# A Perceiver layer on one core: the feed-forward stage in twelve tiles, with its head inside the last closing

## The chip, the cores and the metric

The kernel runs on one core of one Trainium2 chip. The metric is device time in microseconds: 2316.69 us is the median of three runs before the change (2315.12 to 2320.33). A core has five engines with instruction streams of their own: PE (matrix products; its weight loads are listed as PEld), DVE (vector), ACT (scalar functions), POOL (general) and SP, which here issues all DMA transfers. Each engine works through its stream in order. An instruction that waits for another engine or for a DMA holds up all that stand behind it on its own engine, and on SP those are the transfers of other parts of the kernel.

## What is computed

Three blocks on `x` of 16 x 32 tokens by 512, each behind a layer norm and with a residual: a graph block, a state-space scan with 128 heads in 8 groups, and a feed-forward block. The change is about the third. Its weight matrices are a quarter as wide as the layer and are repeated four times, and each has a rank-two addition:

```python
def _qlora_linear(x, wq, A, B):
    w = jnp.tile(wq, (1, 4))
    base = x @ w.T
    lora = x @ A.T @ B.T
    return base + lora * LORA_SCALING               # 0.5
gate = silu(_qlora_linear(x, w1q, a1, b1))      # 512 -> 1376
up = _qlora_linear(x, w3q, a3, b3)              # 512 -> 1376
x = x + _qlora_linear(gate * up, w2q, a2, b2)   # 1376 -> 512
```

Since the weights repeat, `x @ w.T` is the sum of the four quarters of `x`, times the small matrix: one product with 128 rows in place of four.

## The kernel before

**The scan** (`scan_part`, L1116) runs in an order written out by hand (`manual_schedule`, L1258): each engine gets its instructions in the order of the Python code. The loop over groups (L1493) does for each of 8 steps i: the projections of the next group (`gate`, `current`, both through `project`, L1175, whose weights come by SP into six buffers of the tag `win`), and for the present group `turn` (transposes, decays; it also issues the load of a `wo` tile), `outputs` (PE products `py`) and `gated` (DVE, ACT and, on POOL, the sum of squares `ssq`). POOL also makes `da` (`spread`, L1275), which PE needs for `pl` (`decays`). A group ends with a closing: 32 products of 128x512 with the output weights, in four blocks q of 128 tokens, and an addition to `xt` per block (`close`, L1466; for the first six groups `close_by_seven`). `close` yields in the middle and at the end of each block. The closing of group 6 is woven into the steps of group 7; that of group 7 runs by itself.

**The rank-two parts** (`LowRank`, L130) are done in bf16: an f32 operand is split into three bf16 parts (`split`: eight DVE operations), and the products of the parts stand in 18 rows, multiplied by masks (`masks`). `load` fetches and splits the three `b` matrices in ten pieces; it is a generator that `current` advances by one piece per step from the loop of group 0 on. Its first piece makes the masks, issues the loads `lw` on SP (nine per piece) and clears the tiles on POOL; each further one splits the piece before and loads the next.

**The feed-forward stage** (`ffn_part`, L1522) begins when the scan has ended, in pools of its own, and its order is chosen by the framework's scheduler. Its **head**: six weight loads, layer norm of the four blocks of `xt` (ACT's Ln and Exp, each with a table load), 16 transposes, the sum `vs` of the four quarters, and the rank-two products `pa` of the values with `a1` and `a3` (18 columns, 512 tokens) with their splits. Its **tiles**: 16 tiles of 86 hidden units; for each two f32 products (L1580), two bf16 products of the rank-two part (L1589), Silu on ACT, the product on DVE, a third f32 product with `a2` into 18 columns (L1597), and from tile 4 on the addition into one of four sums. Its **output**: the split of the third low-rank sum, 16 f32 products with `w2` and four bf16 ones (L1605, L1606), four additions of the residual (L1608) and four stores.

Of the kernel before, what the change touches and what calls it, by code (L numbers as in the profile page):

```python
# [8 lines left out]
F32 = mybir.dt.float32  # L9
F16 = mybir.dt.float16  # L10
BF16 = mybir.dt.bfloat16
# [32 lines left out]
TG = NT // G_M  # L44
HT = 86
NHT = 16
LR = 18
LEAD = 6
PREP = (49, 46, 42)
# [4 lines left out]
def kernel(ctx: ExitStack, tc: tile.TileContext, I, out):  # L54
# [67 lines left out]
    late = ctx.enter_context(tc.tile_pool(name="late", bufs=1))  # L122
    lows = LowRank(nc, tc, late, I)
    with ExitStack() as cx:
        scan_part(nc, tc, cx, I, id32, ones, xt, U, rstd, lows)
    with ExitStack() as cx:
        ffn_part(nc, tc, cx, I, id32, xt, layernorm, lows, out)


class LowRank:  # L130

    def __init__(self, nc, tc, const, I):
        self.nc, self.tc, self.I = nc, tc, I
        self.weights = {
            n: const.tile([P, w], BF16, name=f"lb{n}") for n, w in (("1", HT * NHT), ("3", HT * NHT), ("2", D))
        }
        self.values = {n: const.tile([P, D], BF16, name=f"lv{n}") for n in ("1", "3", "2")}  # L140

        self.of = [const.tile([LR, 3], F32, name=f"lof{k}") for k in range(2)]

    def masks(self, pool):
        nc = self.nc
        t = pool.tile([LR, 3, 3], F32, name="lmask")
        for k, pat, width in ((0, [[-6, 3], [0, 3]], 6), (1, [[-2, 3], [-6, 3]], 2)):
            nc.gpsimd.memset(t, 1.0)
            nc.gpsimd.affine_select(
                out=t, in_=t, compare_op=ALU.is_ge, fill=0.0, base=0, pattern=pat, channel_multiplier=1  # L150
            )
            nc.gpsimd.affine_select(
                out=t, in_=t, compare_op=ALU.is_ge, fill=0.0, base=width - 1,
                pattern=[[-a, b] for a, b in pat], channel_multiplier=-1,
            )
            if k == 0:
                nc.vector.tensor_copy(self.of[0], t[:, :, 0])
            else:
                nc.vector.tensor_reduce(self.of[1], t, AX.X, ALU.add)

    def split(self, pool, dst, src, of, key):

        nc = self.nc
        n = src.shape[-1]
        for k in range(3):
            p = pool.tile([LR, n], BF16, tag="lp", name=f"lp{key}_{k}")
            nc.vector.tensor_copy(p, src)  # L167
            if k < 2:
                nc.vector.tensor_tensor(src, src, p, ALU.subtract)  # L169
            if k == 0:  # L170
                nc.vector.tensor_scalar(dst, p, of[:, 0:1], None, ALU.mult)  # L171
            else:
                nc.vector.scalar_tensor_tensor(dst, p, of[:, k:k + 1], dst, ALU.mult, ALU.add)  # L173

    def load(self, pool, width=344):
        nc = self.nc
        self.masks(pool)
        for t in (*self.weights.values(), *self.values.values()):
            nc.gpsimd.memset(t, 0.0)
        for n, t in self.weights.items():  # L180
            for c in range(0, t.shape[-1], width):
                cols = slice(c, min(c + width, t.shape[-1]))
                w = pool.tile([LR, width], F32, tag="lw", name=f"lw{n}_{c}")[:, :cols.stop - c]
                for k in range(9):
                    nc.sync.dma_start(out=w[2 * k:2 * k + 2], in_=self.I[f"b{n}T"][:, cols])
                yield
                self.split(pool, t[:LR, cols], w, self.of[1], f"b{n}_{c}")


def node_orders(nc, pool, tmp, ps, X, idx, id32, nid, own, others):  # L190
# [922 lines left out]
            pass  # L1113


def scan_part(nc, tc, cx, I, id32, ones, xt, u, rstd, lows):  # L1116


    sc = cx.enter_context(tc.tile_pool(name="sconst", bufs=1))
# [373 lines left out]
    for g in range(G_M):  # L1493
        mix = Mix(g)
        conv = None
        for i in range(TG):
            if g + 1 < G_M:
                gate(g + 1, i)
            end_of(conv)
            conv = None  # L1500
            if i:
                mix.gated(i - 1)
            mix.turn(i)
            if g + 1 < G_M:
                conv = current(g + 1, i)
                next(conv)
            else:
                next(last, None)
            mix.summed(i)
            mix.outputs(i)  # L1510
# [3 lines left out]
            mix.summed(TG)  # L1514
        end_of(last)
        last = mix.closing()
        if g + 2 != G_M:
            end_of(last)
            last = None


def ffn_part(nc, tc, cx, I, id32, xt, layernorm, lows, out):  # L1522


    fc = cx.enter_context(tc.tile_pool(name="fconst", bufs=1))
    wk = cx.enter_context(tc.tile_pool(name="fwk", bufs=2))
    sm = cx.enter_context(tc.tile_pool(name="fsm", bufs=3))
    ps = cx.enter_context(tc.tile_pool(name="fps", bufs=2, space=PSUM))
    ps1 = cx.enter_context(tc.tile_pool(name="fps1", bufs=1, space=PSUM))
    NH = HT * NHT  # L1530
    w = {}
    for name, shape in (
        ("a1T", [P, 4, 2]), ("a3T", [P, 4, 2]), ("a2T", [HT, NHT, 2]), ("w1T", [P, NH]), ("w3T", [P, NH]),
        ("w2T", [HT, 4, D]),
    ):
        w[name] = fc.tile(shape, F32, name=f"f_{name}")
        nc.sync.dma_start(out=w[name], in_=I[name])
        if name[0] == "a":

            t = fc.tile([shape[0], shape[1], LR], F32, name=f"f_{name}r")  # L1540
            nc.vector.tensor_copy(
                t.rearrange("p k (a r) -> p k a r", r=2),
                w[name].unsqueeze(2).to_broadcast([shape[0], shape[1], LR // 2, 2]),
            )
            w[name] = t

    v = fc.tile([P, 4, D], F32, name="v")
    for q in range(4):
        layernorm(sm, v[:, q], xt[:, q], f"ff{q}")
    vT = fc.tile([P, 4, D], F32, name="vT")  # L1550
    for k in range(4):
        pt = ps.tile([P, 4, P], F32, tag="t", name=f"fpt{k}")
        for q in range(4):
            nc.tensor.transpose(pt[:, q], v[:, q, k * P:(k + 1) * P], id32)  # L1554
        nc.scalar.copy(vT[:, k], pt.rearrange("p q t -> p (q t)"))  # L1555

    vs = fc.tile([P, D], F32, name="vs")
    nc.vector.tensor_tensor(vs, vT[:, 0], vT[:, 1], ALU.add)
    for k in (2, 3):
        nc.vector.tensor_tensor(vs, vs, vT[:, k], ALU.add)  # L1560
    def lower(n, pa):
        t = fc.tile([LR, D], F32, name=f"low{n}")
        nc.vector.tensor_scalar(t, pa, 0.5, None, ALU.mult)  # L1563
        lows.split(wk, lows.values[n][:LR], t, lows.of[0], f"v{n}")

    for n in ("1", "3"):
        pa = ps1.tile([LR, D], F32, tag="lo", name=f"pa{n}")
        for k in range(4):
            nc.tensor.matmul(pa, lhsT=w[f"a{n}T"][:, k], rhs=vT[:, k], start=(k == 0), stop=(k == 3))  # L1569
        lower(n, pa)  # L1570

    gsum = fc.tile([HT, 4, D], F32, name="gsum")
    pa2 = ps1.tile([LR, D], F32, tag="lo2", name="pa2")
    half = []

    def first(t):
        pp = {}
        for n in ("1", "3"):
            pp[n] = ps.tile([HT, D], F32, tag=f"p{n}", name=f"fp{n}_{t}")
            nc.tensor.matmul(pp[n], lhsT=w[f"w{n}T"][:, t * HT:(t + 1) * HT], rhs=vs, start=True, stop=False)  # L1580
        half.append(pp)

    first(0)
    for t in range(NHT):
        if t + 1 < NHT:
            first(t + 1)
        pp = half.pop(0)
        for n in ("1", "3"):
            nc.tensor.matmul(  # L1589
                pp[n], lhsT=lows.weights[n][:, t * HT:(t + 1) * HT], rhs=lows.values[n], start=False, stop=True  # L1590
            )
        sg = wk.tile([HT, D], F32, tag="sg", name=f"sg{t}")
        nc.scalar.activation(sg, pp["1"], AF.Silu)
        r = t % 4
        gt = gsum[:, r] if t < 4 else wk.tile([HT, D], F32, tag="gt", name=f"gt{t}")
        nc.vector.tensor_tensor(gt, sg, pp["3"], ALU.mult)
        nc.tensor.matmul(pa2, lhsT=w["a2T"][:, t], rhs=gt, start=(t == 0), stop=(t == NHT - 1))  # L1597
        if t >= 4:
            nc.vector.tensor_tensor(gsum[:, r], gsum[:, r], gt, ALU.add)
    lower("2", pa2)  # L1600
    for q in range(4):
        tq = slice(q * P, (q + 1) * P)
        po = ps.tile([P, D], F32, tag="t", name=f"fpo{q}")
        for r in range(4):
            nc.tensor.matmul(po, lhsT=gsum[:, r, tq], rhs=w["w2T"][:, r], start=(r == 0), stop=False)  # L1605
        nc.tensor.matmul(po, lhsT=lows.values["2"][:, tq], rhs=lows.weights["2"], start=False, stop=True)  # L1606
        o = wk.tile([P, D], F32, tag="fo", name=f"fo{q}")
        nc.vector.tensor_tensor(o, po, xt[:, q], ALU.add)  # L1608
        nc.sync.dma_start(out=out[tq, :], in_=o)


# [50 lines left out]
```

## Time and profile before

| | |
|---|---|
| median of three runs | 2316.69 us (2315.12 to 2320.33) |
| the profiled execution, first to last instruction | 2316.7 us |
| PE busy | 2131.8 us, 92% |
| DVE busy | 1835.5 us, 79% |
| ACT busy | 1140.4 us, 49% |
| POOL busy | 840.7 us, 36% |
| mean granted clock of PE | 0.977 |
| scan ends, feed-forward stage begins | about 2218 us |
| its first bf16 product | 2249.2 us |

How to read the profile. Its times are from the start of the span. In the timeline a line gives start, duration, engine, source line, operation, output<-inputs, and how many like instructions were merged; in brackets stands how long the engine was idle before and what released it. An f32 product shows as two records. In a table by stretches the columns are: stretch, its length, then the busy time of PE, PEld, DVE, ACT and POOL (with numbers of instructions), the clock granted to PE as a share of full speed, the busy share of the DMA engines, and GB/s. The ends of products are modelled.

### The profile page before, as it was taken

The numbers are of one execution on the slowest core, as the hardware profiler recorded it, in microseconds if no ns is written. First come the engines' busy times: TensorE is split into PE (matmuls) and PEld (weight loads), VectorE is DVE, ScalarE is ACT, GpSimd is POOL, SyncE is SP. The second block draws the span as 40 slices with busy tenths as digits, with TensorE's granted clock in tenths as the row PEclk, the third lists the DMA queues.
The fourth block names the chain that finished last, engine by engine and source line by source line (L and its number), as shares of the span: only waits on it lengthen the run. The fifth ranks groups of instructions, "written<-read, shape, count | busy, mean of one in ns | idle before, by whom it ended". The sixth has DMA issues, their size and how long they took to land. (4 is left out here: it accounts for less than half of the span.)

```text
span 2316.7 us, 89754 instructions
## 1 busy us (share of the span) xinstructions
PE 2131.8 (92%) x39522; PEld 1300.3 (56%) x39522; DVE 1835.5 (79%) x3974; ACT 1140.4 (49%) x2073; POOL 840.7 (36%) x897
## 2 busy tenths in 40 slices
PE   5599899999999998899999789989999999999979
PEld 2255555776557775567777544455646566464422
DVE  8488897999989999889999763788786967866643
ACT  6686667556675554455555222433353534435321
POOL 2156656455565565655655100111120202112200
PEclk9899999999999999999999799999999999999989
DMA  1324242231232322323212112112122121211100
GB/s 46 81 59 84 52 81 60 52 83 45 63 76 48 82 52 49 84 47 77 56 36 44 49 51 79 60 56 89 45 73 64 46 91 55 73 60 46 37 37 18
DMA packets 121629, 138.05 MB, mean 60 GB/s; under 512 B 18398, under 2 KB 79506, under 8 KB 121154
## 3 DMA queue, kind: packets, MB, share of 16 engines
q1 hardware_dynamic: 121240, 132.32, 22.5%
q8 instruction: 311, 5.10, 1.0%
q14 instruction: 78, 0.64, 0.1%
HBM read 77.02 MB, written 12.85 MB: 39 GB/s over the span
## 5 line engine op out<-in xcount | busy, mean ns | idle before, releaser
L890 POOL TENSOR_TENSOR EN<-e,rz 128x480 f32<-128x480 f32 x344 | 342.5, 996 | 499.4 <-DVE rz L888 410.2
L915 PE MATMUL u<-WA,DD 128*32 128x128 bf16 (+1 forms) x16512 | 414.1, 248 | 16.6 <-issue 16.4
L920 ACT COPY us<-u 128x512 f32<-128x512 f32 x516 | 302.1, 587 | 152.3 <-PE u L915 136.9
L915 PEld LDWEIGHTS <-DD 128*32 128x32 f16 x16512 | 338.6, 97 | 50.6 <-issue 48.1
L875 ACT ACTIVATE e<-s,smc 128x480 f32<-128x480 f32 x344 | 227.7, 662 | 252.6 <-PE s L870 222.0
L811 POOL TENSOR_TENSOR DD<-fs,crep 128x480 f16<-128x480 f32 (+2 forms) x344 | 349.6, 1017 | 0.0
L943 PEld LDWEIGHTS h<-e,us 128*32 128x32 f32 (+1 forms) x11008 | 246.0, 125 | 133.4 <-issue 66.6
L943 PE MATMUL h<-e,us 128*32 128x30 f32 (+1 forms) x11008 | 279.2, 210 | 31.3 <-issue 14.0
L1368 POOL TENSOR_TENSOR ssq<-ssq,sq 128x512 f32<-128x512 f32 x56 | 89.9, 1606 | 592.6 <-ACT sq L1367 592.6
L862 DVE TENSOR_REDUCE c<-s 128x16 bf16<-128x480 f32 x344 | 220.5, 641 | 83.8 <-PE s L853 80.4
L1181 PE MATMUL ppg<-hT,wing 128*128 128x512 f32 x512 | 238.3, 609 | 0.0
L1181 PE MATMUL ppch<-hT,winch 128*128 128x512 f32 x512 | 230.5, 592 | 0.0
L896 DVE STREAM_TRANSPOSE e<-EN 128x512 f32<-128x512 f32 x344 | 224.7, 653 | 0.0
L882 DVE TENSOR_REDUCE z<-e 128x16 f32<-128x480 f32 x344 | 219.6, 638 | 0.5 <-ACT e L875 0.4
L1194 DVE SCALAR_TENSOR_TENSOR cyh<-ppch,t_conv_w,cyh 128x496 f32<-128x496 f32 (+2 forms) x192 | 137.5, 716 | 99.9 <-ACT cyh L1188 95.3
L541 ACT ACTIVATE sgn<-kd 128x512 bf16<-128x512 f32 x256 | 153.1, 598 | 51.4 <-PE kd L540 48.3
L853 PEld LDWEIGHTS <-DD 128*32 128x32 f16 x5504 | 80.8, 96 | 158.2 <-issue 135.5
L751 DVE TENSOR_SCALAR oh<-it,rank 128x512 bf16<-128x512 f16 x512 | 155.8, 365 | 8.5 <-PE pp L705 8.5
L853 PE MATMUL s<-DX,DD 128*32 128x120 f16 x5504 | 142.3, 221 | 18.6 <-DMA DX<-DD 15.3
L1181 PEld LDWEIGHTS ppch<-hT,winch 128*128 128x128 f32 x512 | 94.5, 190 | 109.1 <-issue 102.5
L1181 PEld LDWEIGHTS ppg<-hT,wing 128*128 128x128 f32 x512 | 94.5, 192 | 107.0 <-issue 99.4
L870 PE MATMUL s<-c,idb 128*128 128x480 bf16 x344 | 130.4, 379 | 5.6 <-DVE c L862 2.7
(372 smaller groups left out, 3156.1 us busy)
## 6 DMA issues: line engine op xcount, KB each, us to landing
DX<-DD SPq DMA_DIRECT2D x456, 90.0 KB
wing<-in_in_proj SPq DMA_DIRECT2D x64, 256.0 KB
winch<-in_in_proj SPq DMA_DIRECT2D x64, 256.0 KB
wo<-in_out_proj SPq DMA_DIRECT2D x64, 256.0 KB
crep<-dC SPq DMA_DIRECT2D x128, 64.0 KB
dS<-so SPq DMA_DIRECT2D x32, 256.0 KB
fs<-dS SPq DMA_DIRECT2D x128, 64.0 KB
wincB<-in_in_proj SPq DMA_DIRECT2D x8, 256.0 KB
```

The costliest lines, as they stand in the source:

```text
L751: nc.vector.tensor_scalar(oh[:, j], it2, rank[:, c, m, 4 * g + b:4 * g + b + 1], None, ALU.is_equal)
L811: nc.gpsimd.tensor_tensor(d[:, :, m0 - n0:n1 - n0], win, crep[:, :, m0:n1].unsqueeze(3).to_broadcast([P, 4, n1 - m0, K]), ALU.subtract,)
L853: nc.tensor.matmul(s[rh, j * 4 * QB:(j + 1) * 4 * QB].rearrange("p (b q) -> p b q", b=4), lhsT=d[:, h, c0:c0 + 32], rhs=dx[:, h, :, c0:c0 ...
L862: nc.vector.tensor_reduce(c, live["s", at, gi].rearrange("p (i q) -> p i q", q=QB), AX.X, ALU.max, negate=True)
L875: nc.scalar.activation(e, s.rearrange("p (i q) -> p i q", q=QB), AF.Exp, scale=smc)
L882: nc.vector.tensor_reduce(z, e, AX.X, ALU.add)
L890: nc.gpsimd.tensor_tensor(en[:, :, :QB], e, rz.unsqueeze(2).to_broadcast([P, NI, QB]), ALU.mult)
L896: nc.vector.transpose(e.rearrange("p i q -> p (i q)"), en.rearrange("p i q -> p (i q)"))
L915: nc.tensor.matmul(u[rh, jj], lhsT=d[:, h, c0:c0 + 32], rhs=WA[k][:, h].rearrange("p b o -> p (b o)"), start=(jj == 0 and k == 0), stop=(k ...
L920: nc.scalar.copy(us[:, j - jj:j + 1], u)
L943: nc.tensor.matmul(h[r:r + co, pr, q0:q0 + QB], lhsT=us[:, j, b * co:(b + 1) * co], rhs=e[:, 4 * j + b, :QB], start=npair > 1, stop=True, ...
L1181: nc.tensor.matmul(pp, lhsT=w[:, k], rhs=hT[:, k], start=(k == 0), stop=(k == 3))
```

## The change

Four things are done.

1. **Twelve tiles.** The 1376 hidden units are taken as four repeats of 344, each in pieces of 128, 128 and 88 rows (`HC`). A piece c of repeat a is a tile. The four repeats of a piece are added, so the output needs three products per block, not four.
2. **Side by side.** The product with `a2` of the four tiles of a piece goes to four groups of 32 columns, into one bank (`pa2[rows]`), four in a row. The output's rank-two weights are copied to all four row groups. `a1` and `a3` stand in one operand of 64 columns, and the split values of both in one tile (`"13"`), `a3`'s at row 32.
3. **The head per block.** `ffn_part` is gone; a class `Ffn` stays in the scan's pools and in the order by hand. Block q-1 is transposed in the middle of closing block q and its rank-two product is done behind it, followed by the norm of block q. One ACT table with Ln and Exp is loaded ahead.
4. **Early fetches.** `fetch` loads all weights at the start of group 7's loop, into buffers of the scan, and spreads `a1`, `a3`, `a2` on POOL.

The masks and the `"2"` weights are copied to row groups 32, 64 and 96 by SBUF-to-SBUF DMAs on SP. The diff, cut to its core:

```diff
@@ LowRank.masks
+        for of in self.of:
+            for r in (32, 64, 96):
+                nc.sync.dma_start(out=of[r:r + LR], in_=of[:LR])
@@ LowRank.load
                 yield
-                self.split(pool, t[:LR, cols], w, self.of[1], f"b{n}_{c}")
+                self.split(pool, t[at, cols], w, at, self.of[1], f"b{n}_{c}")
+        t = self.weights["2"]
+        for r in (32, 64, 96):
+            nc.sync.dma_start(out=t[r:r + LR], in_=t[:LR])
@@ scan_part, loop over groups
+        if g + 1 == G_M:
+            fetched = fetch(nc, I, wpool, sm)
...
+    nc.scalar.preload_act_table_set("natural_log_exp_and_others")
+    for q in range(4):
+        next(last)
+        if q:
+            ffn.turn(q - 1)
+        next(last)
+        if q:
+            ffn.lower(q - 1)
+        ffn.norm(q)
+    ffn.rest()
+def fetch(nc, I, wpool, sm):
...
+            nc.sync.dma_start(
+                out=t[:, :, :rows], in_=I[f"w{n}T"].rearrange("p (a r) -> p a r", a=4)[:, :, r0:r0 + rows]
+            )
...
+    for c, to, k, rows in row_pieces():
+        nc.sync.dma_start(out=w["2"][c][to], in_=I["w2T"][rows, k])
+        nc.sync.dma_start(out=raw2[to, :, c], in_=by_k[rows, k])
+    a13 = sm.tile([P, 4, 64], F32, tag="osum", name="fa13", bufs=TG // 2)
+    nc.gpsimd.memset(a13, 0.0)
+    for n, at in (("1", 0), ("3", 32)):
...
+        nc.sync.dma_start(out=raw, in_=I[f"a{n}T"])
+        nc.gpsimd.tensor_scalar(
+            a13[:, :, at:at + LR].rearrange("p k (a r) -> p k a r", r=2),
+            raw.unsqueeze(2).to_broadcast([P, 4, LR // 2, 2]), 0.5, None, ALU.mult,
+        )
...
+    nc.gpsimd.memset(a2, 0.0)
+    for c, (_, rows) in enumerate(HC):
+        nc.gpsimd.tensor_scalar(
+            a2[:rows, :, c, :LR].rearrange("p k (a r) -> p k a r", r=2),
+            raw2[:rows, :, c].unsqueeze(2).to_broadcast([rows, 4, LR // 2, 2]), 0.5, None, ALU.mult,
+        )
+class Ffn:
...
+    def turn(self, q):
+        pt = self.bank("m", f"fpt{q}").rearrange("p (k t) -> p k t", k=4)
+        for k in range(4):
+            nc.tensor.transpose(pt[:, k], self.v[:, q, k * P:(k + 1) * P], self.id32)
+        nc.vector.tensor_reduce(self.vs[:, tq], pt.rearrange("p k t -> p t k"), AX.X, ALU.add)
+        nc.scalar.copy(self.vT[:, :, tq], pt)
+    def lower(self, q):
+        pa = self.bank("m", f"fpa{q}")[:64, :P]
+        for k in range(4):
+            nc.tensor.matmul(pa, lhsT=self.w["a13"][:, k], rhs=self.vT[:, k, tq], start=(k == 0), stop=(k == 3))
+        t = self.wk.tile([P, D], F32, tag="sq", name=f"flow{q}")[:64, :P]
+        nc.scalar.copy(t, pa)
+        self.lows.split(None, self.lows.values["13"][rows, tq], t, rows, self.lows.of[0], f"v{q}", self.part[:, :P])
+    def rest(self):
...
+        early, late = slice(0, 3 * P), slice(3 * P, D)
+        for t in range(2):
+            first(t, early, True)
+        self.turn(3)
+        nc.scalar.preload_act_table_set("silu_and_others")
+        for t in range(2):
+            first(t, late, False)
+        self.lower(3)
...
+        for t, (a, c) in enumerate(tiles):
+            for f, ph in zip(("1", "3"), pp):
+                nc.tensor.matmul(
+                    ph, lhsT=lows.weights[f][:, cols], rhs=lows.values["13"], start=False, stop=True,
...
+            if t + 2 < len(tiles):
+                first(t + 2, slice(0, D), True)
+            nc.scalar.activation(sg, pp[0], AF.Silu)
+            nc.vector.tensor_tensor(gt, sg, pp[1], ALU.mult)
...
+            if t + 1 == len(tiles):
+                base(0, 0)
+                base(0, 1)
+            for b, x in enumerate(gts):
+                rows = slice(32 * b, 32 * b + 32)
+                nc.tensor.matmul(
+                    pa2[rows], lhsT=w["a2"][:n, b, c], rhs=x, start=(c == 0), stop=(c == len(HC) - 1),
...
+            for x in gts[1:]:
+                nc.vector.tensor_tensor(gts[0], gts[0], x, ALU.add)
...
+        nc.scalar.copy(low, pa2)
+        lows.split(None, lows.values["2"], low, everything, lows.of[0], "v2", self.part)
+        base(1, 0)
...
+        base(1, 2)
+        for q in range(2, 6):
+            if q < 4:
+                for c in range(len(HC)):
+                    base(q, c)
+            for q in {2: (), 3: (0, 1), 4: (2,), 5: (3,)}[q]:
+                finish(q)
```

`first(t, ...)` makes the two f32 products of tile t in banks of the tags `p` and `y` (two each); `base(q, c)` is an f32 product with `w2`; `finish(q)` is the bf16 product, DVE's addition of the residual into a tile of the tag `ssq` (two buffers) and the store.

## Prediction

> **What bounds the kernel now.** The page's span, 2316.7 us, is that of the profiled execution, and the median of the runs shown, 2316.69 us, agrees with it, so every sum below is made against 2316.7. I read first the chain of waits that ended last: on its last 87 us it stands on PE in the feed-forward lines (L1580, L1589, L1597, L1605), before that on ACT and DVE. The busy times by stretch say what that means.
>
> ```profile
> 2200.00:2210.00 10.00, 10.00 (x25) 4.50 (x24) 1.50 (x2) 0.00 (x0) 0.00 (x0) 1.00 0.00 0
> ...
> 2220.00:2230.00 10.00, 1.80 (x6) 0.86 (x6) 4.58 (x27) 9.10 (x14) 0.00 (x0) 0.65 0.45 169
> 2230.00:2240.00 10.00, 8.11 (x20) 2.62 (x20) 3.93 (x9) 3.53 (x5) 0.00 (x0) 0.67 0.10 44
> ...
> 2260.00:2270.00 10.00, 9.93 (x26) 2.65 (x24) 3.40 (x6) 2.15 (x4) 0.00 (x0) 1.00 0.00 0
> ```
>
> PE (the first busy time) is full in the last closing and in the sixteen tiles, and nearly empty in the head between them, where ACT is full and the granted clock falls to 0.65. The timeline gives the tiles:
>
> ```profile
> 2261.23 1.03 PE L1589 MATMUL fp<-lv,lb 128*86 128x512 bf16 x4
> 2261.65 1.08 ACT L1593 ACTIVATE sg<-fp 86x512 f32<-86x512 f32 x2 [5.74 <-PE fp L1589]
> 2262.27 1.28 DVE L1596 TENSOR_TENSOR gt<-sg,fp 86x512 f32<-86x512 f32 x2 [5.54 <-PE fp L1589]
> 2262.29 1.09 PE L1580 MATMUL fp<-vs,f_w1T 128*86 128x512 f32 x2
> 2263.31 1.03 PE L1597 MATMUL pa<-gt,f_a2Tr 86*18 86x512 f32 x2
> ...
> 2268.05 1.03 PE L1589 MATMUL fp<-lv,lb 128*86 128x512 bf16 x4
> ```
>
> Two tiles take 6.82 us (2261.23 to 2268.05). An f32 product is two records of 0.43 us, a bf16 one a record of 0.215; a change between the 128x128 and the 18-column form costs 0.16 or 0.10 (2262.29 to 2263.31 is 1.02, not 0.86). Each tile pays a full 0.86 us product for 18 columns. Measured from S = 2189.10, where the last closing begins, the end is 127.6 us away: 28.6 closing, 31.5 head (to the first L1589 at 2249.16), 50 tiles, 17.5 output.
>
> **The change: the tail.** Blocks 1 to 3 of the closing now carry the head. Behind block q's last matmul PE does the rank-two product of q-1 (0.16 + 4 x 2 x 0.107 = 1.02), ACT copies it (0.28, by the 0.59 of a 512-column copy), DVE splits it (eight operations: 2.07 us at 168 columns from 1603.56, about 1.85 at 128 by the slope to 344), and only then runs block q's norm, 2.92 us as in the chain of 1313.65 to 1316.57 that has no table load. From the block's end: 1.02 + 0.23 drain + 0.3 + 1.85 + 2.92 + waits = 6.4. PE meanwhile has 1.02 and half a block (3.44 + 0.1), so it idles 1.9, then does four transposes (0.53) and the other half (3.44): 10.4 us a block where 6.87 stood. Block 0 ends at S + 6.97; the root, now without its 1.28 table load, and the first norm are ready at S + 13.3, so block 1 ends at S + 17.5, block 3 at S + 38.3. Behind it the last norm (6.3), transposes, sum of four (0.65), the late quarter of two tiles (0.86), the product, copy and split give 12.0: the first bf16 product comes at S + 50.3, where it stood at S + 60.1.
>
> Twelve tiles replace sixteen. But both of a tile's banks come from pools of two, and each tile's bf16 products are followed at once by the f32 products of tile t+2, which need the bank that tile t's Silu reads. By the rows above Silu starts 0.42 after the bf16 product, lasts 0.58, and PE starts 0.06 later: 1.06 instead of 0.43. The old order put two tiles' bf16 products there, and the wait was 0.04. A tile is 1.06 + 1.72 + 0.07 = 2.85; ten of them 28.5. DVE's products and additions (0.69 each, 4.8 us per four tiles) lie beside PE's 13.8; were that cover gone, each addition would cost its 0.69. The Silu table load (1.28) lies behind the last copy of the transposes, while PE does the late quarter.
>
> The rank-two sums run four side by side in 32-column groups. The nearest row is L1352, f32 on two groups of 64 columns: 16 records in 1.03 us (2151.56 to 2152.59) where 0.107 each would make 1.71. I read it as an overlap of neighbours in program order: a group's second record waits for its first, and the next group starts beside it. Four products then take five records, 2.15; ends are two records (0.87) and eight (3.44). With 0.26 of form changes, two of them give 4.8, then two bf16 products and two products of the output (2.8). From the third group on: 2.15, six f32 products around DVE's additions, six more, bf16, 11.4 in all; the split (4.2) lies beside these. Together 50.3 + 28.5 + 4.8 + 2.8 + 11.4 = 97.8 to the first output addition.
>
> The Trainium skill, "TensorE: Matmul & The Clock Gate", Part 3, gives packed tiles one product's span plus 4 ns for each further tile; by it a group is about 0.87 and the sum 3.8 us lower, an estimate; the same page says that matmuls start and end strictly in order, and no row here shows four f32 groups.
>
> The four additions now come in a row, and the output tile has two buffers. In the trace the third addition waited 3.4 us for the first store, which landed 4.4 after its issue; the last store took 3.0 when alone. So: two additions 1.4, the second pair from 5.1 on, 1.4, and a store among two, 3.5: 10.1. End: S + 107.9, 19.7 us earlier.
>
> Less the clock: between block 3 and the tiles PE has 2.2 us of work in 8.4. A similar hole cost:
>
> ```profile
> 1597.55 0.43 PE L1352 MATMUL py<-el,hd 128*64 128x128 f32 x2 [1.57 <-DVE el L1333]
> 1599.21 1.97 PE L1352 MATMUL py<-el,hd 128*64 128x128 f32 x14 [1.24 <-DVE el L1333]
> 1601.11 5.69 PE L1181 MATMUL ppg<-hT,wing 128*128 128x512 f32 x8
> ```
>
> The last line is 3.60 elsewhere. I take 2.5 (ends 0 and 7, if each block loses some): the tail gains **17.2**.
>
> **The change: the front.** Three edits add waits to in-order queues. SP before:
>
> ```profile
> 1446.81 2.71 SPq L185 DMA_DIRECT2D lw<-in_b1T  x9
> 1449.56 0.35 SPq L1343 DMA_DIRECT2D wo<-in_out_proj  x1
> 1450.02 0.38 SPq L1178 DMA_DIRECT2D winch<-in_in_proj  x1
> ...
> 1479.87 3.08 SPq L185 DMA_DIRECT2D lw<-in_b1T  x9
> ```
>
> The last line shows SP standing 18 us for DVE's split. `masks` now issues six copies on SP, just ahead of the nine at 1446.81, and they read what DVE writes here:
>
> ```profile
> 1467.86 0.15 DVE L157 COPY lof<-lmask 18x3 f32<-18x3 f32 x1
> ...
> 1468.73 0.15 DVE L159 TENSOR_REDUCE lof<-lmask 18x3 f32<-18x9 f32 x1 [0.73 <-POOL lmask L152]
> ...
> 1470.66 0.59 PE L1181 MATMUL ppch<-hT,winch 128*128 128x512 f32 x1
> ```
>
> Behind them stands the load that PE uses at 1470.66. SP gets on at 1468.0: 6 x 0.3, nine loads 2.7, one wo 0.4, issue at 1473.0; two loads of 256 KB at some 290 GB/s (the rate of 2182) land about 1476.3. PE stands 5.6 and then, cold, 1.7 more: **7.3** (ends 4 and 10). The three copies of the "2" weights do the same behind the split that ends at 1605.70: issue at 1607.2, landing 1610.2, needed at 1607.94: **2.3** (ends 0 and 4). DVE waits for PE in both places, so nothing makes it up.
>
> `fetch` puts its loads behind the last projection (2137.83). Twenty issues end near 2143.8 and land near 2146 (small a1 load: under 2.6 us to its reader). Its seven POOL instructions stand between these two:
>
> ```profile
> 2143.56 1.64 POOL L1368 TENSOR_TENSOR ssq<-ssq,sq 128x512 f32<-128x512 f32 x1 [6.98 <-ACT sq L1367]
> ...
> 2145.16 1.07 POOL L1278 TENSOR_TENSOR da<-lei,dA 128x512 f32<-128x512 f32 x1
> ...
> 2146.29 1.13 PE L1288 MATMUL pl<-da,gt 128*128 128x512 f32 x2 [0.48 <-POOL da L1278]
> ```
>
> Two memsets and five small operations by POOL rows of 0.2 to 0.5 make 2.2, and 0.4 of waiting for the loads: `da`, then `pl`, then the whole closing come **2.6** later (ends 0 and 6). The loads themselves hide: the queue was idle from 2111 to 2179 (uncovered, their 2.1 MB at 290 GB/s are 7 us). The changed shapes of the split weights (rows, not columns) and the POOL memsets in `load` cost nothing: the columns stay, and POOL idles there (one memset of 0.51 goes, two of about 0.1 come).
>
> Sum: 2316.7 - 17.2 + 7.3 + 2.3 + 2.6 = **2311.7**.
>
> **Rivals.** (1) SP's copies don't hold the loads: with 7.3 and 2.3 gone it is 2302.1. For it: only that such copies were not seen; against it, the line at 1479.87. (2) Slower: POOL in the last group waits for `fetch`'s pieces. Six of them have runs of 8 bytes; each us that the last lands after 2146 is a us on the path. It decides from 9.6 us (landing 2155.7); PE once waited 15.3 for a small-piece DX load, and 14 would give 2326. Against it: only 11 KB are so cut. (3) The sums don't run side by side: 8 records, 3 x 1.29 more, 2315.6; with the clock held low in each block 2320.
>
> **Chances.** A measurement of this kernel tells about 0.2% (4.6 us) from no change: faster is below 2312.1, slower above 2321.3. The forecast, with its own range 2305 to 2318, has 0.60, of which 0.33 lies below 2312.1; rival 1 has 0.18, rival 2 0.10, rival 3 0.12. Faster 0.51, same 0.39, slower 0.10. The range goes from rival 1's 2302 to rival 3's 2320.
>
> **What would show it.** First bf16 product 50 us after the closing's start; 2.85 us a tile with PE released by Silu; three idle pieces of 1.9 before the transposes; the third output addition waiting for a store; SP's six copies directly behind the DVE reduction of L159 and PE standing some 6 us for winch; `pl` 2 to 3 us later behind `da`. Wrong if winch is already there, if the tiles run at 2.2, or if the last group starts more than 5 us later.

## The result, and the profile after

The changed kernel takes 2339.78 us (median of 4 runs, 2335.46 to 2345.99) where the kernel before took 2318.51 in the runs beside it: the ratio is 1.0091, with a 95% interval of 1.0070 to 1.0111. It is slower by 0.9%, and lies above the predicted range. The profiled execution of the changed kernel (2338.14 us) has a span of 2336.2 us, 19.5 more than before.

To place these 19.5 us I compared the start of every `da` on POOL (31 in the scan) in the two traces. Between stalls the distance stays the same to 0.01 us, so each step in it belongs to one place:

| place | distance to before, us | step | predicted |
|---|---|---|---|
| first groups (the code ahead of them is unchanged) | 0.92 | 0.92 | 0 |
| copies of the masks on SP, 1469 to 1485 | 11.04 | +10.1 | +7.3 (4 to 10) |
| pieces of `b3` and the closing at 1555 | 13.61 | +2.6 | 0 |
| copies of the "2" weights, 1619 to 1632 | 20.26 | +6.65 | +2.3 (0 to 4) |
| `fetch`, 2131 to 2190 | 37.72 | +17.5 | +2.6 (0 to 6) |
| from the last closing to the end | 19.5 | -18.2 | -17.2 |

The first line is no effect of the change: in the profiled executions below, the unchanged part ahead of the scan ends between 1.8 us earlier and 6.0 us later than before. Distances below are taken from that mark.

**The tail did what was forecast.** In the table by stretches (stretch, length, busy PE, PEld, DVE, ACT, POOL, granted clock, DMA share, GB/s) the hole in PE is gone but for a part:

```profile
2240.00:2250.00 10.00, 9.76 (x27) 4.71 (x28) 3.96 (x12) 0.84 (x2) 0.00 (x0) 0.83 0.00 0
2250.00:2260.00 10.00, 8.03 (x28) 3.82 (x27) 4.88 (x17) 1.25 (x4) 0.00 (x0) 1.00 0.00 0
...
2270.00:2280.00 10.00, 5.47 (x24) 4.09 (x23) 4.31 (x16) 2.53 (x5) 0.00 (x0) 0.83 0.01 2
```

The nearly empty stretch of before (1.80 of 10 us) has no counterpart; the weakest is the one with the last norm (5.47). The timeline of PE shows a tile, the rank-two sums and the first output:

```profile
2285.73 0.59 PE L1690 MATMUL fp<-lv,lb 128*128 128x512 bf16 x2
2286.80 1.98 PE L1651 MATMUL fp<-fvs,fw 128*128 128x512 f32 x4 [0.47 <-ACT sg L1697]
2288.62 0.59 PE L1690 MATMUL fp<-lv,lb 128*128 128x512 bf16 x2
...
2294.49 1.06 PE L1708 MATMUL fpa<-fg,fa2r 128*32 128x512 f32 x8
...
2298.37 1.12 PE L1651 MATMUL fp<-fvs,fw 128*128 128x512 f32 x2 [0.68 <-DVE fg L1699]
```

A tile takes 2.89 us (2285.73 to 2288.62), and PE is released by Silu's `sg`, as predicted (2.85). Eight records of the rank-two sums take 1.06 us.

**The front gave more than that back.** SP and then PE at the masks:

```profile
1468.95 4.75 SPq L165 DMA_DIRECT2D lof<-lof  x6
1473.81 2.75 SPq L193 DMA_DIRECT2D lw<-in_b1T  x9
1476.60 0.36 SPq L1354 DMA_DIRECT2D wo<-in_out_proj  x1
1477.07 0.36 SPq L1189 DMA_DIRECT2D winch<-in_in_proj  x1
```
```profile
1480.11 5.19 PE L1192 MATMUL ppch<-hT,winch 128*128 128x512 f32 x8 [8.38 <-DMA winch<-in_in_proj]
```

Six copies of 216 bytes occupy SP for 4.75 us, then come nine loads and `wo`; `winch` is issued at 1477.07 and PE, which wanted it at 1471.7, gets it 8.38 us late and then runs cold, that is, at a granted clock of 0.50 from 1480 to 1483 (5.19 us for 3.60). The "2" weights repeat it in small:

```profile
1619.39 2.28 SPq L198 DMA_DIRECT2D lb<-lb  x3
...
1621.72 0.47 SPq L1354 DMA_DIRECT2D wo<-in_out_proj  x1
...
1622.61 0.33 SPq L1189 DMA_DIRECT2D winch<-in_in_proj  x1
...
1626.33 5.47 PE L1192 MATMUL ppch<-hT,winch 128*128 128x512 f32 x8 [5.85 <-DMA winch<-in_in_proj]
```

Stall and cold product are 7.7 us here; the step in the table is 1.1 less, because the projection ahead of it was cold for longer before than after (5.69 and 4.48). Last, `fetch`, on SP, POOL and PE:

```profile
2148.74 9.93 SPq L1567 DMA_DIRECT2D fw<-in_w3T  x3
2158.71 0.47 SPq L1575 DMA_DIRECT2D fw<-in_w2T  x1
2159.23 0.74 SPq L1576 DMA_DIRECT2D fa<-in_a2T  x1
2160.01 5.18 SPq L1575 DMA_DIRECT2D fw<-in_w2T  x1
...
2171.52 5.28 SPq L1583 DMA_DIRECT2D fa<-in_a1T  x1
```
```profile
2165.42 0.30 POOL L1580 MEMSET fa<- 128x256 f32 x1
2178.28 0.86 POOL L1584 TENSOR_SCALAR fa<-fa 128x72 f32<-128x72 f32 x2 [12.56 <-DMA fa<-in_a1T]
...
2180.63 1.07 POOL L1289 TENSOR_TENSOR da<-lei,dA 128x512 f32<-128x512 f32 x1
```
```profile
2181.75 2.08 PE L1299 MATMUL pl<-da,gt 128*128 128x512 f32 x2 [15.67 <-POOL da L1289]
2183.62 4.95 PE L1482 MATMUL po<-wo,gs 128*128 128x512 f32 x8
```

POOL arrives at 2165.42, as before on the shifted clock (the time of before and the distance of the table: 2145.16 + 20.26). There it stands 12.56 us for a load that SP issued last but one; `da`, `pl` and the last group stand behind it. The three loads of `w3` stretch over 9.93 us only because SP waited for their buffers, which PE's last projections freed one by one (a single issue is 0.54). The long single issues, 5.18 and 5.28, are something else, which e6 takes up.

### The profile page after: what moved, and what is told of

It reads as the page before. It is cut to its first block, busy times and chain, and to the rows that moved or that the text cites. A ratio compares the mean times of both kernels' runs of the same rounds, so it can differ in the third digit from the quotient of the medians.

```text
span 2336.2 us, 89751 instructions
## 1 busy us (share of the span) xinstructions
PE 2110.4 (90%) x39506; PEld 1300.5 (56%) x39506; DVE 1835.0 (79%) x3978; ACT 1130.9 (48%) x2067; POOL 842.7 (36%) x905
```

## The experiments

**Each of the three front edits alone, and all three.** What a run gains over the changed kernel is a difference of medians taken at different times; the kernel before took 2317.9 to 2320.1 us beside them, so the step that the trace shows at the place is given too. The copies of the masks (but one) and of the "2" weights are issued ahead of the last closing, and POOL's seven instructions (`widen`) stand behind the last group; `spread_masks` issues the copies of the masks and rows that it is given:

```diff
@@ e1, LowRank.masks
-        for of in self.of:
-            for r in (32, 64, 96):
-                nc.sync.dma_start(out=of[r:r + LR], in_=of[:LR])
@@ e1, LowRank.load, ahead of the third piece
+                    self.spread_masks([(1, 32)])
@@ scan_part, ahead of Ffn: e1 the other five copies, e2 the three copies of "2", e3 POOL's part of fetch
+    lows.spread_masks([(0, 32), (0, 64), (0, 96), (1, 64), (1, 96)])
+    lows.spread_twos()
+    widen(nc, fetched, sm)
```

> Against the changed kernel, 2339.8. Five of the six copies of the masks are issued ahead of the last closing, and the one that the splits need ahead of the third piece of loads, when its source has long been written. Theory (SP's order): the copies' wait for DVE and their 4.75 us of issue held back the load winch, so PE's stall of 8.38 and the cold projection behind it go: 10.1 less, and 2.3 more if the closing at 1555 keeps its clock: 2327 to 2330. Rival (winch is late anyway, because SP next stands for DVE's split, as it did for 18 us in the kernel before): 2337 to 2340.

Measured: 2329.01 us (ratio to before 1.0048, 1.0034 to 1.0062), 10.8 less than the changed kernel. In the trace `winch` stalls PE once, not twice; the front up to 2128 is 10.6 us shorter. The closing at 1555 stays cold all the same, so the extra 2.3 did not come.

> Against the changed kernel, 2339.8. The three copies of the 2 weights are issued ahead of the last closing. Theory (SP's order): PE's stall of 5.85 at 1626 and the 1.87 by which the projection behind it is cold go: 2332. Rival (what I predicted, the copies only cost their issue and the load was nearly late anyway): 2336 to 2338.

Measured: 2329.33 us (1.0056, 1.0039 to 1.0073), 10.5 less; the trace gives 7.6 of it to this place, which is the theory's 7.7, the rest is within the spread of the runs (2326.8 to 2339.0). The copies still run, only later: it was their place that cost.

> Against the changed kernel, 2339.8. Loads stay where they are; only the seven POOL instructions of the fetch stand behind the last group's loop. Theory (POOL's order: da stands behind instructions that wait for the late small loads): the 15.2 us by which da is late and the 2.3 of a cold closing go: 2322. Rival (the loads themselves, their traffic or SP's 18 us of issues, hold the last group): above 2334.

Measured: 2322.87 us (1.0019, 1.0005 to 1.0033), 16.9 less. The loads are where they were, and `da` is on time:

```profile
2166.72 1.65 POOL L1379 TENSOR_TENSOR ssq<-ssq,sq 128x512 f32<-128x512 f32 x1 [6.98 <-ACT sq L1378]
2168.33 1.07 POOL L1289 TENSOR_TENSOR da<-lei,dA 128x512 f32<-128x512 f32 x1
```

That is the pair of lines of before again, `da` directly behind `ssq`. The traffic of the loads costs nothing here. Of the 17.5 us of this place 15.9 went with the wait on POOL; the 1.6 left are a cold stretch behind it, of which more below.

> All three moves together. Theory: the three stalls lie one behind the other on PE's path, so they add up: 10.1 to 12.4, 7.7 and 17.5, 35 to 38 less, 2302 to 2305, faster than the kernel before by 14 to 17. Rival (where PE gets its loads earlier it runs into DVE, which was in step with it before the change): a third of the gain is lost, 2314.

Measured: 2306.32 us (0.9943, 0.9924 to 0.9962): 33.5 less, somewhat under the theory's 35 to 38, and faster than before by 0.6%. The traces give 10.6, 7.6 and 15.9 for the three places alone, and 33.9 for all three here, so the three add up. In its trace the last `da` is 2.9 us behind before (from the common mark), against 36.8. Of the 2.9, 1.3 come in the closing at 1555 and the projection behind it, and 1.64 at 2167, where three products run cold behind holes of 1.42 and 1.18 us that before had too, without going cold. The same stretch costs 1.4 to 1.6 in every run from e1 to e9, and nothing in the changed kernel; I have no cause for it.

**Taking the masks' 10.1 us apart.**

```diff
         for of in self.of:
-            for r in (32, 64, 96):
-                nc.sync.dma_start(out=of[r:r + LR], in_=of[:LR])
+        self.spread_masks([(1, 32)])
```

> Against the changed kernel, 2339.8. Of the six copies of the masks one stays in its place, ahead of the first loads; five are issued ahead of the last closing. It parts the masks' 10.1 us into the wait for DVE and the copies' own issue. Theory (five issues of 0.8 us are 4.0 of the 8.38 that PE stood, and the rest is SP's wait for DVE's masks, which one copy suffers too): PE still stands 4.4 us for winch, 2335.8. Rival (the issues lie beside the loads' own time, only the wait counts): PE still stands 8, 2339.

Measured: 2335.46 us (1.0059, 1.0035 to 1.0082), 4.3 less by the medians and 3.0 by the trace. PE's stall:

```profile
1470.72 0.87 SPq L169 DMA_DIRECT2D lof<-lof  x1
...
1474.94 0.36 SPq L1193 DMA_DIRECT2D winch<-in_in_proj  x1
```
```profile
1477.98 5.19 PE L1196 MATMUL ppch<-hT,winch 128*128 128x512 f32 x8 [5.35 <-DMA winch<-in_in_proj]
```

From SP's first copy to `winch` it is now 4.22 us, not 8.12: five issues less are 3.90. The stall falls by 3.03 only, since the copy left over reads the second mask, written 0.87 later than the first, at which six copies could begin. Five issues are 3.0 of the 10.1 us; the rest is the wait for DVE with what was queued behind it, and the cold product.

**Which loads made `fetch` late.** In e5 the lines of `fetch` are reordered: a1 and a3, then the six pairs of w2 and a2, and w1 and w3 last. e6 leaves out the loads of `a2` (six, with pieces of 8 bytes) and POOL clears the tile instead.

```diff
@@ e6, fetch
+    nc.gpsimd.memset(raw2, 0.0)
...
-        nc.sync.dma_start(out=raw2[to, :, c], in_=by_k[rows, k])
```

> Against the changed kernel, 2339.8. In the fetch the loads of a1, a3, w2 and a2 stand ahead of those of w1 and w3; POOL's seven instructions stay ahead of da. Theory (the small loads were late because SP first stood, in order, for the six buffers of w1 and w3, the last of them free at 2158, and then needed 18 us to issue fourteen loads): they are issued from 2131 on and have landed when POOL gets there at 2165; da is 2.3 late for the seven instructions, and 13 of the 15.2 us go: 2326. Rival (the seven instructions or the small pieces hold POOL wherever the loads stand): above 2335.

Measured: 2326.35 us (1.0031, 1.0015 to 1.0047), the theory's value; by the trace the last `da` is 11.9 less late. POOL waits for no load any more:

```profile
2166.94 0.76 POOL L1568 TENSOR_SCALAR fa<-fa 128x72 f32<-128x72 f32 x2
2167.62 0.42 POOL L1581 MEMSET fa2r<- 128x384 f32 x1
2168.13 1.43 POOL L1583 TENSOR_SCALAR fa2r<-fa 128x72 f32<-128x72 f32 x3
2169.53 1.06 POOL L1289 TENSOR_TENSOR da<-lei,dA 128x512 f32<-128x512 f32 x1
```

Its seven instructions make `da` 3.0 us late. This is the case that I had predicted for the change as it stands (2.6).

> Against the changed kernel, 2339.8. Leaves out the six loads of a2, whose pieces are 8 bytes long; its tile is cleared by POOL instead, so the third low-rank sum is zero. Theory (8-byte pieces fill SP's queue, and SP stands 5.2 us twice for them): the issues behind 2158.7 take 6 x 0.5 and a1 lands before POOL gets there: 13 less, 2326. Rival (the pieces of 512 bytes of w1 and w3 fill the queue, or the 5.2 us belong to w2 and a1 themselves): SP's long issues stay, and only 6 x 0.8 go, 2335.

Measured: 2331.78 us (1.0054, 1.0036 to 1.0072), between the two. SP and POOL:

```profile
2160.92 2.32 SPq L1576 DMA_DIRECT2D fw<-in_w2T  x6
2163.29 0.52 SPq L1583 DMA_DIRECT2D fa<-in_a1T  x1
```
```profile
2172.47 0.76 POOL L1584 TENSOR_SCALAR fa<-fa 128x72 f32<-128x72 f32 x2 [4.49 <-DMA fa<-in_a1T]
```

Both long issues are gone: `a1`'s is 0.52, not 5.28, and so is the 5.18 among `w2`'s. So they need the 8-byte pieces, and they are paid by the load behind these on SP. The number of pieces does not explain them, though. The six pairs of `w2` and `a2` have 86, 42, 44, 84, 2 and 86 rows; only behind the two pairs of 86 rows (344 pieces of `a2` each) does the next issue stand. Behind the pair of 84 rows (336 pieces) it took 0.43 in the changed kernel:

```profile
2168.18 0.88 SPq L1576 DMA_DIRECT2D fa<-in_a2T  x1
2169.10 0.43 SPq L1575 DMA_DIRECT2D fw<-in_w2T  x1
```

What differs is how `w2`'s rows of 2 KB move. In the trace's records of DMA packets of the changed kernel, the first load of 86 rows takes from 2160.4 to 2164.7, the one of 84 rows from 2168.7 to 2169.9. By stretches, the two loads of 86 rows (the first two lines) and the same in e6 (the third):

```profile
2161.00:2164.00 3.00, 2.34 (x7) 0.78 (x6) 2.97 (x6) 2.71 (x4) 0.17 (x1) 1.00 0.12 43
2173.00:2176.00 3.00, 0.00 (x0) 0.00 (x0) 0.00 (x0) 0.00 (x0) 0.00 (x0) 0.50 0.13 48
```
```profile
2166.00:2171.00 5.00, 2.10 (x20) 1.46 (x20) 3.79 (x6) 2.36 (x4) 1.95 (x3) 1.00 0.13 50
```

A DMA share of 0.13 is about two of the sixteen engines. The first 344 pieces of `a2` move only behind these rows, from 2164.5 to 2165.8, and SP's issue of 5.18 ends among them, at 2165.19.

In e6 `a1` still lands 9.2 us after its issue, and POOL still waits 4.49. The same records tell what for: the loads of `w3`, ahead of it in the queue, have moved by 2162.7; of the 256 pieces of `a1` and `a3`, 224 move from 2164.4 to 2165.2 and the other 32 at 2171.4 to 2171.7, just as `w2`'s last rows end (2171.6). So a load of 4 KB waits for the rows of 2 KB that stand ahead of it on about two engines. From the change to here `da` is 8.1 us less late (15.2 to 7.1); of the 7.1, 4.5 are this wait. No run divides the 86 rows differently, so what that alone would give is not shown; e5, with `a1` issued ahead of them, has no wait for it.

The Trainium skill ("Perfetto Trace Analysis", "DMA Instruction — HWDGE (DVE, Sync)") says that the profiled time of an issue is waiting for and using the descriptor generator, without the movement of the data, and that the engines start early when there are more descriptors than the buffer holds. Long issues that vanish with the smallest pieces agree with that; no run here shows the buffer itself.

**The tiles.** On top of the three moves, e7 puts the bf16 products of two tiles together; e8 also adds each tile to its sum directly behind its product and gives the output four buffers.

```diff
@@ e7, Ffn.rest, loop over tiles
+            for u in (t, t + 1) if t % 2 == 0 else ():
...
@@ e8
-            for x in gts[1:]:
-                nc.vector.tensor_tensor(gts[0], gts[0], x, ALU.add)
+            if a:
+                nc.vector.tensor_tensor(gsum[:n, c], gts[0] if a == 1 else gsum[:n, c], gt, ALU.add)
...
-            o = wk.tile([P, D], F32, tag="ssq", name=f"fo{q}")
+            o = wk.tile([P, D], F32, tag=("ssq", "cy")[q // 2], name=f"fo{q}", bufs=(2, 3)[q // 2])
```

> The version with all three moves (2306.3 in its runs), and in the tiles the bf16 products of two tiles stand together, so that a pair's f32 products follow both. Theory (my step: 1.06 us from a tile's bf16 product to the next f32 product, since that needs the bank that Silu reads): a pair takes 1.06 + 0.1 + 3.44 = 4.7 us where two tiles took 5.78; five pairs, 5 us less: 2301. Rival (the second bank is freed by DVE's product, 0.7 later than Silu, so the wait only moves): 2305.

Measured: 2296.30 us (0.9903, 0.9881 to 0.9925), 10.0 less than e4, of which the trace gives 6.1 to the tiles: from the first bf16 product to the end it is 54.98 us in e4 and 48.85 here, and some 0.9 of these 6.1 is a first tile less cold (3.68 for 1.98 there, 4.47 for 3.70 here), which leaves 5.2 for the pairs. The other 3.9 us of the medians are spread. Two tiles:

```profile
2252.93 1.03 PE L1713 MATMUL fp<-lv,lb 128*128 128x512 bf16 x4
2253.99 3.70 PE L1671 MATMUL fp<-fvs,fw 128*128 128x512 f32 x8
2257.62 1.06 PE L1731 MATMUL fpa<-fg,fa2r 128*32 128x512 f32 x8
```

4.69 us a pair (4.7 expected), and no line names Silu.

> The pairs, and besides: DVE adds each tile to its sum directly behind its product, not three in a row behind the rank-two sums, and the output has four buffers. Theory: the f32 product that waited 0.68 for DVE twice no longer does, the last addition's 0.29 goes, and the third output addition does not wait 1.6 for a store: 3 us less than the pairs alone, 2298. Rival (the two last stores now stand on each other in the queue and land when they did): 1 us less, 2300.

Measured: 2293.45 us (0.9896, 0.9871 to 0.9920), 2.9 less than e7; the intervals overlap, but the trace has 45.71 us for the same stretch, 3.1 less. The output no longer waits for a store:

```profile
2294.94 2.48 DVE L1699 TENSOR_TENSOR fo<-fpo,xt 128x512 f32<-128x512 f32 x4 [3.88 <-PE fpo L1697]
```

With e8 the feed-forward change is 1.0% faster than the kernel before.

## Why the prediction was wrong

**The step that failed** is "Twenty issues end near 2143.8 and land near 2146 (small a1 load: under 2.6 us to its reader)". Six of the twenty went out earlier, as buffers came free, and the start of the other fourteen was right (the last projection, 2158 on the shifted clock), but I priced each at a row of 0.3 us for loads with long pieces. Behind 2158.7 they took 18.5 us; `a1` was there at 2178.28, or 2158.0 on the clock of before, 12 us later than I had it. This place holds 14.9 of the 24.5 us between the forecast and the profiled execution (5.0 faster against 19.5 slower). It is the second rival ("POOL in the last group waits for `fetch`'s pieces"), and its point, a landing at 2155.7, was passed. I gave it 0.10 because "only 11 KB are so cut": the bytes did not decide it. What did, by the packet records above, were loads of 86 rows that move on about two DMA engines, with 8-byte pieces behind them; I had priced all loads by one rate. Of the 15.2 us by which `da` was late, the runs give 8.1 to the 8-byte loads, 4.5 to `a1`'s landing behind `w2`'s rows (e6) and the remaining 2.6 to POOL's own instructions (3.0 in e5). Behind `pl` 2.3 us more are lost to the clock.

**The masks:** the mechanism was right in every link: SP got on at 1468.95 (predicted 1468.0, plus the 0.92), the landing came 3.04 after the issue, the projection behind was cold by 1.6. The term that was mis-sized is the six copies: 4.75 us against 6 x 0.3. That is 2.95 us more, and accounts for the 2.8 by which the step was short. **The "2" weights:** the same 0.76 a copy (2.28 in all, I had 1.5 to the issue of `winch` and it was 3.3, with the `wo` load that I left out), a landing after 3.7 and not 3.0, and a cold product of 1.87 that I did not count: 6.65, not 2.3. The first rival, that the copies hold nothing, fell with e1 and e2.

**The changed shapes** were to cost nothing. In the pieces of `b3`, which now lie at partition 32, the DVE rows start and end 0.1 us later each (0.22 a piece), and PE's wait for `el` grows from 0.73 to 0.99. The rest of the 2.6 us comes because the closing at 1555 begins cold. It does so in all versions but e5, where the same waits (0.98 and 1.25 for 0.99 and 1.24) stand ahead of it and the whole step is 1.0. The changed kernel and e5:

```profile
1554.85 2.08 PE L1449 MATMUL po_p<-wo,gs 128*128 128x256 f32 x4
```
```profile
1556.78 1.13 PE L1449 MATMUL po_p<-wo,gs 128*128 128x256 f32 x4
```

So some 1.6 of the 2.6 us are a cold start that the shapes alone do not bring about. Whether partition 32 is the cause of the other 1.0 was not tried.

**The tail:** -18.2 against -17.2, from errors that cancel. The first bf16 product came 54.7 us behind the closing's start (50.3, and 2.5 for the clock): the second half of block 1 took 5.29 cold, and the late quarter and the last rank-two product were cold as well. From there to the first output addition it was 47.5, as summed. Within it the staircase of 2.15 us was wrong: all four products overlap and the eight records take 1.06. The Trainium skill's rule ("TensorE: Matmul & The Clock Gate", Part 3), which I weighed and did not take, agrees with it (an estimate by that rule is 0.87, and a change of form). But DVE's three additions then made a tile wait 0.68 twice, which I had counted as hidden. The output took 7.2, not 10.1: the third addition waited 1.60, not 3.7 from the second's end. Two slips of the prediction change nothing in this: the projection of 5.69 us takes 3.70 elsewhere, not 3.60, and the term of 11.4 us names twelve f32 products where the code has ten; 11.4 is what ten give, and it measured 10.7.

## What to carry to other kernels

A DMA issue has a price on its queue's engine that goes by the shape of the load and by what was issued just ahead of it, not by the bytes: read it from a row of the same shape, and list what stands behind it. Look in the trace at how many DMA engines a load keeps busy: here 86 rows took 4.3 us and 84 rows 1.2. An instruction put ahead of a wait in an in-order queue takes all of that wait for those behind it; ask for each moved load and each helper on an idle engine when its input lands, and put it behind the work with a due time. A gain at the end of a kernel and small stalls at its front are worth the same on one path, so a version that keeps the first and moves the second can turn the sign.

## What the runs showed of the hardware

- A copy of 216 bytes or 18 KB from SBUF to SBUF on 18 partitions occupies SP for 0.70 to 0.90 us; a load of 256 KB in long pieces for 0.33 (one of `wo` right behind another load for up to 0.98, in e3), and one of 512-byte pieces for 0.54 to 0.65.
- A load of 86 rows of 2 KB moved at a DMA share of 0.12 to 0.13 and 43 to 50 GB/s; one of 84 such rows moved in 1.2 us, not 4.3.
- A load with pieces of 8 bytes is issued in 0.7 to 0.9 us. Behind one of 344 pieces that follows such a load of 86 rows, the next load's issue takes 5.0 to 5.4; behind one of 336 pieces that follows 84 rows it takes 0.43, and without these loads 0.25 to 0.52.
- Four f32 products in groups of 32 columns, eight records, take 1.06 us, about as long as one product of 512 columns (0.86).
- PE went cold behind holes of 1.4 and 1.2 us in some executions and not in others: single cold stretches of 1.4 to 1.9 us come and go between versions whose order there is the same. Below some 2 us a trace of one execution cannot tell an edit from that.
